# Handing the row maxima of an attention softmax to the padded q by transfers of one element per partition

## The chip, the cores and the metric

The kernel runs on one core of a Trainium2 chip. A core has five engines that each work through their own queue of instructions: PE (the matrix unit; its weight loads are listed apart as PEld), DVE (vector), ACT (activations and copies), POOL and SP, which here only issues transfers. Sixteen DMA engines move the data. The engines meet at semaphores. The metric is the device time of one execution in microseconds; lower is better.

## The reference

The input x has 8 sequences of 1024 tokens with 256 features. Two blocks follow each other, each with a layer norm before and after and a residual around it:

```python
x = x + layernorm(attention(layernorm(x), Wq, Wk, Wv, Wo))
x = x + layernorm(experts(layernorm(x), router, gate_up, down, biases))
```

The attention has 16 heads of 16 features, is causal and scales the scores by 1/4:

```python
score = where(causal, q @ k.T / 4, -inf)      # per sequence and head, 1024 x 1024
attn  = softmax(score, axis=-1)
out   = attn @ v
```

The second block sends each token to the best 2 of 8 experts (512 inner features). It is not touched by the change.

## The kernel before, in words

**Two stages.** The attention stage runs to about 1340 us, the expert stage after it. The change lies wholly in the first.

**Turns.** A turn u is one sequence b and one group g of four heads: 8 x 4 = 32 turns, `b, g = divmod(u, NG)`. The four heads lie on the partitions in bands of 32 rows: `qP` (the padded q) and `kP` hold in each band 16 rows of features and, in row 16 (`hh * HS + DH`), one row more. In `kP` that row is 1. In `qP` it is first 0 and later minus the maximum of each query's scores, so that the same matmul that makes the scores also subtracts the maximum. There are three such pairs of buffers, taken in turn (`u % NU`).

**Two passes over the scores.** The softmax needs each query's maximum before the exponentials. The first pass (`maxima_tiles`, matmul at line 831, tile `sa`) makes the scores with the queries on the partitions, 128 queries a block, eight blocks a turn, and reduces them to maxima on DVE (lines 841 to 866, 885) in the tile `mx`. The second pass (`values_tiles`, line 926, tile `sb`) makes them again with the keys on the partitions, now with the maximum in row 16; ACT takes the exponential (line 938, `pT`), POOL masks the diagonal blocks, PE multiplies by the values (line 967, `av`).

**Steps.** Each pass has nine steps k (`STEPS`, lines 773 to 784), and the loop at line 1309 runs the first pass of turn u and the second pass of turn u - 1 side by side, step by step, in two halves (a pair of heads each). Queries come in two chunks c of 512 (four blocks each). All first-pass scores of chunk 0 are done with step 2. Of chunk 1, blocks 4 to 6 are done with step 7 and block 7 with step 8, the last. The second pass of the next turn reads chunk 0's row at its step 0 and chunk 1's row in the second part of its step 2.

**From maxima to rows.** Between lies `rows(c)` (line 794): DVE takes the last maximum over three partial ones and negates it (line 797, `nm`, 128 queries x 4 heads x 4 blocks), PE transposes that into 16 partitions of 128 (line 800, `nmps`), ACT copies it to SBUF (line 802, `nmT`), and four transfers on SP's queue (line 804) put four rows of 128 for each head into row 16 of that head's band.

**Who orders the work.** In this stage the order on PE, DVE, ACT and SP is the order in which the program emits it. The matmuls of the steps stand fixed; everything else is a job that yields pieces with a cost per engine, and `pump` (line 1250) emits a piece after each half step if its engines have credit. `rows` is an urgent job, begun by `counted_off` (line 870) when the last step of its chunk is done; whatever is not yet emitted when the second pass needs it is forced out at lines 1312 to 1314. `after=1` holds a piece back for one half step more.

**SP's queue.** SP works strictly in order: a transfer that waits holds all behind it. Besides the rows it issues `spread` (lines 754 to 766: two transfers of zeros into the rows 16 of a band and eight that spread q and k into a pair of buffers, for the next turn), the outputs of `normalize` into `aT` (line 1007, four for each turn and chunk), the loads of x, the stores of the first block's result (line 1049), and in the last turn four early loads for the expert stage (`load_early`, line 1280). A transfer also waits until the eighth before it has landed, since eight semaphores go round. `finish` multiplies `aT` by the output weights (line 1028, `yps`).

## Time and profile before

| | us |
|---|---|
| median of 13 runs | 2152.26 (2148.81 to 2157.28) |
| the profiled execution | 2153.21 |
| its span | 2151.5 |
| PE busy | 2069.8 (96%) |
| DVE busy | 1668.1 (78%) |
| ACT busy | 1070.2 (50%) |
| POOL busy | 1051.3 (49%) |
| transposes of the maxima (line 800) | 64 at 0.277 |
| copies of them (line 802) | 64 at 0.249 |
| issues of row transfers on SP (line 804) | 256 at 0.578 |

The profile is of one execution. A group's line names the source line, engine, operation, the tiles written and read, the count and the durations in ns. A line of the time line gives the start, the duration in us, the instruction, how many were merged, and in brackets how long its engine sat idle before it and what ended that. On SP the duration is that of the issue alone; the data move after it.

### The profile page before, as it was taken

What the parts mean: (1) busy time and instruction counts of PE and PEld (TensorE: products, weight loads), DVE (VectorE), ACT (ScalarE), POOL (GpSimd) and SP (SyncE); (2) the same over time, 40 slices, a digit from 0 to 9 for tenths busy, and PEclk for the clock granted to TensorE, in tenths of its full rate; (3) what the DMA queues carried; (4) which work ended last, traced back from release to release, by engine and by line L of the source; (5) the groups of instructions that cost most, each with busy time, mean ns of one, the idle gap of its engine ahead of it and who ended that gap; (6) DMA issues with size and microseconds to landing.
All of it is one profiled execution on the core that took longest, in us unless ns stands there. A gap on an engine that the chain in (4) does not pass through costs nothing.

```text
span 2151.5 us, 44512 instructions
## 1 busy us (share of the span) xinstructions
PE 2069.8 (96%) x16269; PEld 1272.5 (59%) x16269; DVE 1668.1 (78%) x3834; ACT 1070.2 (50%) x2132; POOL 1051.3 (49%) x1216
## 2 busy tenths in 40 slices
PE   7999999999999999999999999899999999999995
PEld 4344444444444444445444444688888888888884
DVE  4676887878786888798787798378778888877776
ACT  3566665666666666666666666333122323232222
POOL 3321563474274365556455355455544445444443
PEclk9999999999999999999999999999999999999998
DMA  4102102112111121211211111656876877777774
GB/s 129 19 9 49 27 29 69 40 35 50 37 48 43 40 58 40 58 46 39 57 39 46 29 54 44 209 179 223 265 248 232 280 273 257 256 243 247 268 278 147
DMA packets 147095, 254.85 MB, mean 118 GB/s; under 512 B 21504, under 2 KB 106008, under 8 KB 144952
## 3 DMA queue, kind: packets, MB, share of 16 engines
q1 hardware_dynamic: 133128, 217.01, 32.9%
q0 software_dynamic: 12528, 34.36, 4.3%
q8 instruction: 130, 2.13, 0.4%
q14 instruction: 93, 0.76, 0.1%
q10 hardware_dynamic: 1216, 0.58, 0.1%
HBM read 171.13 MB, written 55.63 MB: 105 GB/s over the span
## 4 chain that ended last, share of the span: by engine, by line
PE 76%; DVE 13%; POOL 5%; issue 2%; DMA 2%; ACT 2%; SPq 0%; ACTq 0%; DVEq 0%; POOLq 0%
PE sa L831 20%; PE gu L1458 14%; PE av L967 12%; PE dn L1498 8%; PE sb L926 7%; PE yps L1028 3%; PE pjk L738 3%; PE pjq L738 3%; PE vps L724 3%; DVE acc L1573 1%; POOL ytd L1511 1%; DVE act L1479 1%; DVE gate L1467 1%; DVE up L1471 1%; PE xtps L1436 1%
## 5 line engine op out<-in xcount | busy, mean ns | idle before, releaser
L938 ACT ACTIVATE pT<-sb 128x512 f32<-128x512 f32 x1134 | 616.4, 595 | 363.8 <-PE sb L926 347.4
L926 PE MATMUL sb<-qP,kP 32*128 32x512 f32 (+3 forms) x3072 | 710.5, 522 | 3.3 <-DMA qP<-nmT 3.0
L831 PE MATMUL sa<-kP,qP 32*128 32x512 f32 (+3 forms) x3072 | 651.6, 523 | 9.5 <-DVE mx L841 3.8
L1458 PE MATMUL gu<-xsT,wg 128*128 128x256 f32 (+1 forms) x2208 | 487.7, 374 | 6.0 <-DMA wg<-_L_ffn_gate_up_proj_dram 4.1
L1458 PEld LDWEIGHTS gu<-xsT,wg 128*128 128x128 f32 x2208 | 410.1, 191 | 60.6 <-issue 4.8
L947 POOL TENSOR_SCALAR_AFFINE_SELECT pT<-pT 128x512 f32<-128x512 f32 x256 | 161.0, 644 | 500.7 <-ACT pT L938 475.5
L847 DVE TENSOR_REDUCE mx<-sa 128x2 f32<-128x1024 f32 x256 | 311.5, 1219 | 98.6 <-PE sb L926 93.1
L1469 ACT ACTIVATE sig<-gate 128x256 f32<-128x256 f32 (+1 forms) x276 | 112.8, 409 | 533.1 <-DVE gate L1467 528.5
L831 PEld LDWEIGHTS sa<-kP,qP 32*128 32x128 f32 x3072 | 226.8, 184 | 209.5 <-issue 88.8
L967 PE MATMUL av<-pT,vpad 128*32 128x256 f32 (+1 forms) x5120 | 347.8, 367 | 1.1 <-DVE avs L978 0.9
L1474 POOL TENSOR_TENSOR sig<-sig,gate 128x256 f32<-128x256 f32 (+1 forms) x276 | 198.1, 721 | 258.1 <-ACT sig L1469 256.1
L926 PEld LDWEIGHTS sb<-qP,kP 32*128 32x128 f32 x3072 | 299.9, 184 | 39.8 <-ACT pT L938 10.8
L967 PEld LDWEIGHTS av<-pT,vpad 128*32 128x32 f32 x5120 | 115.8, 109 | 290.9 <-issue 220.9
L1498 PE MATMUL dn<-wd,act 128*128 128x256 f32 x1064 | 258.9, 382 | 17.7 <-DVE act L1479 17.1
L1498 PEld LDWEIGHTS dn<-wd,act 128*128 128x128 f32 x1064 | 194.4, 190 | 51.0 <-DVE act L1479 29.1
L1467 DVE TENSOR_SCALAR gate<-gu,bs 128x256 f32<-128x256 f32 (+1 forms) x276 | 129.0, 468 | 121.4 <-PE gu L1458 95.6
L841 DVE CUSTOM_DVE_ANT_0 sa<-sa,cmask 128x512 f32<-128x512 f32 x256 | 178.2, 698 | 53.9 <-PE sb L926 35.5
L1511 POOL DMA_INDIRECT ytd<-ys,places x133 | 133.8, 1006 | 126.1 <-DVE ys L1506 94.0
L1191 POOL DMA_INDIRECT xsd<-xn,slots x128 | 128.1, 1001 | 48.3 <-issue 30.4
L1479 DVE SCALAR_TENSOR_TENSOR act<-up,sig 128x256 f32<-128x256 f32 (+1 forms) x276 | 125.7, 455 | 25.1 <-POOL sig L1474 25.1
L885 DVE TENSOR_REDUCE mx<-edge 128x8 f32<-128x1024 f32 x96 | 116.0, 1208 | 20.5 <-POOL edge L880 20.3
L866 ACT COPY edge<-sa 128x512 f32<-128x512 f32 x192 | 113.1, 589 | 34.1 <-DVE mx L862 20.0
(244 smaller groups left out, 2327.0 us busy)
## 6 DMA issues: line engine op xcount, KB each, us to landing
wg<-_L_ffn_gate_up_proj_dram SPq DMA_DIRECT2D x69, 1024.0 KB
wd<-in_L_ffn_down_proj_dram SPq DMA_DIRECT2D x69, 512.0 KB
xs<-xsd SPq DMA_DIRECT2D x60, 258.0 KB
yy<-ytd SPq DMA_DIRECT2D x15, 1024.0 KB
bs<-biasd SPq DMA_DIRECT2D x69, 132.0 KB
x<-in_L_attn_x_dram SPq DMA_DIRECT2D x16, 512.0 KB
aT<-avn SPq DMA_DIRECT2D x256, 32.0 KB
x1d<-y SPq DMA_DIRECT2D x16, 512.0 KB
```

The lines of the kernel that those rows point to most:

```text
L831: nc.tensor.matmul(ps[:, hh, ds(at, w)], lhsT=qP[r, ts(i, P)], rhs=kP[r, ds(c * QC, w)], start=True, stop=True,)
L841: nc.vector.tensor_tensor_reduce(out=ps[:, hh, :], in0=ps[:, hh, :], in1=cmask, scale=1.0, scalar=NEG, op0=ALU.add, op1=ALU.max, accum_out ...
L847: nc.vector.tensor_reduce(mx[:, heads, i, 2:3], ps, AX.X, ALU.max)
L926: nc.tensor.matmul(banks[hh][:, ds(at, QC - off)], lhsT=kP[r, ts(j, P)], rhs=qP[r, ds(c * QC + off, QC - off)], start=True, stop=True,)
L938: nc.scalar.activation(pT[:, 2 * pair + hh, :], banks[hh], AF.Exp)
L947: in_order(nc.gpsimd.affine_select(out=d, in_=d, compare_op=ALU.is_ge, fill=0.0, base=0, pattern=[[0, HG], [1, P]], channel_multiplier=-1,))
L967: nc.tensor.matmul(av[ds(hh * HS, HS), ds(off + a - at, z - a)], lhsT=vp[:, j, ds((g * HG + hh) * VS, HS)], rhs=pT[:, hh, a:z],  start=c n ...
L1458: nc.tensor.matmul(ps[:, half, :w], lhsT=wg[:, kt, ds(half * FF + f * P, P)], rhs=xT[:, kt, :], start=(kt == 0), stop=(kt == KT - 1),)
L1467: nc.vector.tensor_scalar(gt, ps[:, 0, :w], bs[:, f : f + 1], LIMIT, ALU.add, ALU.min)
L1474: in_order(nc.gpsimd.tensor_tensor(sg, sg, gt, ALU.mult))
L1498: nc.tensor.matmul(pss[n][:, 0, :], lhsT=act[:, f, ts(n, P)], rhs=wd[:, f, :], start=(f == 0), stop=(f == FT - 1),)
L1511: put = nc.gpsimd.indirect_dma_start(out=yt_dram[:, :], out_offset=bass.IndirectOffsetOnAxis(ap=places[:, i, n : n + 1], axis=0), in_=y[:, ...
```

## The change

`rows` now works on three groups in place of two chunks: chunk 0, blocks 4 to 6 of chunk 1, and block 7. It no longer transposes. After the reduction (`nm`, 128 queries on 128 partitions) each block of each head leaves by a transfer of its own that takes one 4-byte element from each of 128 partitions and puts them side by side into row 16: 16 transfers for chunk 0, 12 and 4 for chunk 1. The transpose, its PSUM tile, the copy and the tile `nmT` are gone, and so is the half step for which the second piece was held back. The first of chunk 1's groups is begun after step 7, the other after step 8. `rows_of` holds a list of jobs for each chunk.

```diff
--- before.py
+++ after.py
@@ -791,27 +791,32 @@
             mx = mxs[u % 2]
             edges = {}
 
-            def rows(c):
+            def rows(group):
+                c, blocks = GROUPS[group]
                 yield piece(dve=0.2)
-                nm = ap2.tile([P, HG, n], F32, tag="nm", name=f"nm_{u}_{c}")
-                nc.vector.tensor_reduce(nm, mx[:, :, ts(c, n), :], AX.X, ALU.max, negate=True)
-                yield piece(pe=0.15, act=0.3, after=1 if u else 4)
-                ps = ps_b.tile([HG * n, P], F32, tag="b", name=f"nmps_{u}_{c}")
-                nc.tensor.transpose(ps, nm.rearrange("p h i -> p (h i)"), ident)
-                nmT = ap2.tile([HG * n, P], F32, tag="nmT", name=f"nmT_{u}_{c}")
-                nc.scalar.copy(nmT, ps)
-                for hh in range(HG):
-                    nc.sync.dma_start(
-                        out=qP[hh * HS + DH : hh * HS + DH + 1, ts(c, QC)].rearrange(
-                            "o (i q) -> o i q", q=P
-                        ),
-                        in_=nmT[ts(hh, n), :],
-                    )
-
-            left = [
-                sum(c in {i // n for i, _, _ in tiles} for _, tiles, _ in STEPS)
-                for c in range(NC)
-            ]
+                m = len(blocks)
+                nm = ap2.tile([P, HG, m], F32, tag=f"nm{m}", name=f"nm_{u}_{group}")
+                nc.vector.tensor_reduce(
+                    nm, mx[:, :, ds(c * n + blocks[0], m), :], AX.X, ALU.max, negate=True
+                )
+                yield piece()
+                for i in range(m):
+                    for hh in range(HG):
+                        r = hh * HS + DH
+                        nc.sync.dma_start(
+                            out=qP[r : r + 1, ds(c * QC + (blocks[0] + i) * P, P)],
+                            in_=nm[:, hh, i : i + 1],
+                        )
+
+            GROUPS = [(0, range(n)), (NC - 1, range(n - 1)), (NC - 1, range(n - 1, n))]
+
+            def groups_of(k):
+                return {
+                    g for g, (c, blocks) in enumerate(GROUPS)
+                    if any(i // n == c and i % n in blocks for i, _, _ in STEPS[k][1])
+                }
+
+            left = [sum(g in groups_of(k) for k in range(K)) for g in range(len(GROUPS))]
 
             def of_two(k):
 
@@ -868,10 +873,12 @@
                 return scores, reduce
 
             def counted_off(k):
-                for c in {i // n for i, _, _ in STEPS[k][1]}:
-                    left[c] -= 1
-                    if not left[c]:
-                        rows_of[u, c] = start(urgent, rows(c))
+                for g in sorted(groups_of(k)):
+                    left[g] -= 1
+                    if not left[g]:
+                        rows_of.setdefault((u, GROUPS[g][0]), []).append(
+                            start(urgent, rows(g))
+                        )
 
             def masked_edges(k):
 
@@ -1310,8 +1317,9 @@
                     if second:
 
                         for c in {t[0] for t in STEPS[k][2]}:
-                            while not rows_of[u - 1, c].done:
-                                emit(urgent, rows_of[u - 1, c])
+                            for job in rows_of[u - 1, c]:
+                                while not job.done:
+                                    emit(urgent, job)
                     if u == B * NG - 1 and not early and NT - LATE in known:
                         load_early()
                     if first and g == 0 and b + 1 < B and k == 5:
```

## The prediction

> **What bounds the kernel now.** I read the page first (busy shares, groups, DMA issues), then the table by stretch, then the instructions of the tiles nm, nmps and nmT, the chain, and last the time line around one handing-over of maxima.

> ```profile
> span 2151.5 us, 44512 instructions
> PE 2069.8 (96%) x16269; PEld 1272.5 (59%) x16269; DVE 1668.1 (78%) x3834; ACT 1070.2 (50%) x2132; POOL 1051.3 (49%) x1216
> ...
> PE 76%; DVE 13%; POOL 5%; issue 2%; DMA 2%; ACT 2%; SPq 0%; ACTq 0%; DVEq 0%; POOLq 0%
> ```
> ```profile
> 400.00:700.00 300.00, 295.24 (x2857) 140.13 (x2852) 240.28 (x497) 191.31 (x369) 163.98 (x179) 1.00 0.18 44
> 700.00:1000.00 300.00, 297.24 (x2850) 140.68 (x2848) 248.83 (x551) 189.00 (x367) 166.31 (x180) 1.00 0.19 47
> ```
> The columns are stretch, length, then PE, PEld, DVE, ACT, POOL busy, granted clock, DMA share, GB/s. In the attention stage (to about 1340 us, 32 turns of about 41 us) PE is busy for 98 to 99%, at full clock. Time taken from PE is time taken from the stage; time added to anything else costs only where it makes PE wait. The expert stage after it is not touched.

> What the change removes, and what the removed transfers cost:
> ```profile
> L797 DVE TENSOR_REDUCE nm<-mx x64: 158/200/204, 41.0 to 1331.7; 128x16 f32<-128x48 f32 x64
> L800 PE MATMUL nmps<-ident,nm x64: 269/277/278, 45.3 to 1332.5; 128*16 128x128 f32 x64
> L802 ACT COPY nmT<-nmps x64: 236/249/255, 45.6 to 1333.2; 16x128 f32<-16x128 f32 x64
> L804 SPq DMA_DIRECT2D qP<-nmT x256: 572/578/722, 45.9 to 1335.6; - x128
> ```
> Other transfers to compare the new ones with (min/median/max ns that SP is held for one issue): three from SBUF to SBUF, one from SBUF to DRAM in 1024 pieces of 32 bytes, one of 128 rows from DRAM:
> ```profile
> L759 SPq DMA_DIRECT2D qP<-zeros x58: 565/600/649, 88.5 to 1255.1; - x58
> L762 SPq DMA_DIRECT2D qP<-unq x132: 526/583/1668, 17.8 to 1257.7; - x132
> L1007 SPq DMA_DIRECT2D aT<-avn x256: 507/582/2742, 85.9 to 1373.5; - x128
> L693 SPq DMA_DIRECT2D biasd<-bias x1: 527/527/527, 37.0 to 37.0; - x1
> L1419 SPq DMA_DIRECT2D bs<-biasd x69: 332/346/1832, 1358.9 to 2110.4; - x69
> ```
> One handing-over, turn 6, from three answers of the time line (DVE, SP, weight loads):
> ```profile
> 294.69 1.23 DVE L847 TENSOR_REDUCE mx<-sa 128x2 f32<-128x1024 f32 x1 [0.68 <-PE sb L926]
> ...
> 298.43 1.23 DVE L847 TENSOR_REDUCE mx<-sa 128x2 f32<-128x1024 f32 x1 [0.44 <-PE sb L926]
> 299.69 0.20 DVE L797 TENSOR_REDUCE nm<-mx 128x16 f32<-128x48 f32 x1
> ```
> ```profile
> 302.14 2.66 SPq L804 DMA_DIRECT2D qP<-nmT  x4
> ```
> ```profile
> 309.29 0.19 PEld L926 LDWEIGHTS sb<-qP,kP 32*128 32x128 f32 x2
> ```
> The seventh block's maxima (step 7) end at 295.92, the eighth's at 299.66; the rows are issued from 302.14 to 304.80 and first read at 309.29, 13.4 us after the end of step 7. Read the same way, the first read comes 10.9 to 14.7 us after step 7 in turns 1 to 30 (six of them within 10.9 to 11.1). Only in turns 0 and 31 do the weight loads wait long for the rows; the last wait shows how late a row lands, 1.08 us after the last issue ended at 1336.17:

> ```profile
> 69.07 0.49 PEld L926 LDWEIGHTS sb<-qP,kP 32*128 32x128 f32 x2 [3.38 <-DMA qP<-nmT]
> ...
> 1337.25 0.29 PEld L926 LDWEIGHTS sb<-qP,kP 32*128 32x128 f32 x2 [0.37 <-DMA qP<-nmT]
> ```

> **The change part by part.**

> *PE, off.* 64 transposes. 64 x 0.277 = 17.7 us is the upper end. In the chain from 296 to 345 us line 800 holds 1.3% of 49 us, 0.64 us for three transposes: 0.21 us each, as their start overlaps the matmul before. 64 x 0.21 = 13.4 us is the lower end while PE stays the bound. I take 14.

> *ACT, off.* 64 copies, 15.9 us. ACT is busy for 63 to 64% of this stage, and its copy lay beside PE's work: 0. Should PE's queue ever wait for ACT there, it is a gain of under 1 us.

> *DVE, on.* Three reductions in place of two a turn. By 0.20 us for 48 elements and 0.158 at the least, the two smaller ones take 0.15 to 0.19 each: +0.15 us a turn, 4.8 us busy. DVE holds 13% of the chain: +0.6 us; ends 0 and 4.8.

> *SP, on.* 256 issues become 1024: 16 for chunk 0, then 12 and 4 for chunk 1. By the four SBUF-to-SBUF rows an issue holds SP for 0.578 to 0.600 us; the bounds are 0.346 (128 rows from DRAM) and 0.722 (the worst of line 804). I take 0.59, since the new ones are SBUF to SBUF too. SP then issues some 204 transfers in four turns, 120 of 166 us: it is no bound as a whole, but the bursts matter.

> *Chunk 1 (the tight one).* The instruction order of the new program puts group 1's reduction right behind the last one of step 7, and both groups ahead of the next spread of q and k, behind which the old rows stood. Group 1 can be issued 0.6 us after step 7 (a 0.2 us reduction and hand-overs). Twelve issues end at 0.6 + 12 x 0.59 = 7.7 us; group 2's maxima are ready at 3.7 to 5.1, so its four follow at once and end at 10.0. With 1.08 us to land, the rows are there 11.1 us after step 7: on time in every turn, by 3.6 us at most and by nothing in the six tight ones (a head read 0.2 us later needs the last issue; that makes up for the 0.2 us that PE comes earlier). The lateness against the read, summed over turns 1 to 30 (0.6 + 16 issues + 1.08, less the read): nothing at 0.58 us an issue, 1 at 0.60, 9 at 0.65, 21 at 0.70, 34 at 0.75, 97 at 0.90. I take +1. The turns that end a batch start group 1 behind the spread of ten transfers; for turn 11 (chunk 0 from 486.1: 16 + 4 + 10 issues end at 504.3) the rows land at 514.8, the read is at 515.7.

> *Waits that go.* PE and its loads now wait 8.8 us, eight times, for the rows, 4.1 of it (3.38 and 0.72) in turn 0, whose rows stood behind a spread. There step 7 ends at 55.4, so the new rows land at 66.5 in place of 69.07: -2.6 us. I take -3, ends 0 and -8.8.

> *Turn 31.* Here the new order puts the four early loads of the expert stage between groups 1 and 2; they took 3.76 us of SP before. Rows then land at about 1328.0 + 7.1 + 3.8 + 2.4 + 1.08 = 1342.4 instead of 1337.25: +5 us, ends 0 and +10.

> *Behind chunk 0.* Its 16 issues are queued ahead of aT's four. In turn 4 they end at 197.3 + 9.6 = 206.9 instead of 202.1, so aT is out at 209.3; its projection starts at 211.7, 1.3 us after the landing. The other fifteen projections have 3.2 to 17 us. Cost 0; from 0.7 us an issue on it is no longer nothing. The spread that follows has half a turn and more: 0.

> *Landing.* The one thing the trace has no row for is 128 pieces of 4 bytes that go into one partition. L693's 1024 pieces of 32 bytes started within 0.73 us, so 128 need about 0.1 us; its packets took 7.8 ns each. If instead all 128 went in one after the other, it would be 1.0 us: landing 1.0 later, some 11 us of waits at 0.59. I take 0, ends 0 and +11.

> [...]

> Sum: -14 + 0.6 + 1 - 3 + 5 = -10.4. The profiled execution took 2153.2 us (span 2151.5), 0.9 above the median of 2152.3. 2153.2 - 10.4 = 2142.8; against the median 2141.9. I say 2142.

> **The rivals.**

> *Cheap issues.* An issue takes the 0.346 us of L1419. Then no row is ever late: -17.7 - 8.8 + 0.6 = 2127. For it: equally 128 pieces. Against: every SBUF-to-SBUF row is at 0.58.

> *Hidden.* PE's free slots fill with other waits, because DVE (80 to 83% busy) sets the pace of those steps: 2152. For it: DVE's 13% of the chain. Against: PE's 98 to 99%.

> *Slow landing.* One partition takes the pieces singly, or landing grows by 1.6 us: 19 us of waits, 2142 + 19 = 2161.

> *SP late (the slower side).* The issue of an element-wise transfer is dearer than of any row here. It decides at about 0.65 us: there waits cancel the gain. At 0.75 it is 2142 + 33 = 2175, at 0.90 2238, and by 0.82 (50 issues in 41 us) SP is the bound of the stage. For it: the chunk-1 margin is 0 in six turns. Against: L693, at 0.527 for 1024 pieces.

> **How the numbers follow.** Forecast 0.45 (its own range 2134 to 2149), cheap issues 0.15, hidden 0.10, slow landing 0.10, SP late 0.20, half of it above 2185. The range 2126 to 2185 leaves out that half and a twentieth below. This kernel's measurement can tell about 0.2% (4.3 us) from no change. Faster: 0.42 + 0.15 = 0.57; same: 0.03 + 0.08 = 0.11; slower the rest, 0.32.

> **What would show it.** Right: PE has 64 matmuls fewer, its busy share of the stage stays at 98%, SP's new issues are at 0.55 to 0.62 us, and sb's waits for qP stay under 10 us in all. Wrong: SP's element-wise issues over 0.65 us, waits of PE on qP from nm in most turns, waits of yps for aT, or a landing over 2 us after the issue's end.

## The result, and the profile after

The changed kernel takes 2201.24 us (median; 2198.5 to 2206.4), the kernel before beside it 2151.08 us. The ratio is 1.0234, with a 95% interval of 1.0222 to 1.0245: slower, by 2.3%. The prediction was 2142 us with a range to 2185; sign and range are both missed. The profiled execution's span grew from 2151.5 to 2201.5 us, so the +50.0 us can be followed in the trace.

The page of the kernel after: span, busy time of each engine, and the shares of the chain that ended last.

```profile
span 2201.5 us, 45760 instructions
PE 2082.1 (95%) x16205; PEld 1277.6 (58%) x16205; DVE 1670.2 (76%) x3866; ACT 1063.7 (48%) x2068; POOL 1053.9 (48%) x1216
...
PE 68%; DVE 15%; POOL 7%; issue 3%; DMA 3%; SPq 2%; ACT 1%; ACTq 0%; DVEq 0%; POOLq 0%
```

PE ran 64 matmuls fewer, as it should, and was nevertheless busy for 12 us more. In the chain, DMA and SP's queue have gone from 2% to 5%. The two stretches that the prediction showed, and then two short ones (length, then busy time of PE, PEld, DVE, ACT, POOL, granted clock, DMA share, GB/s):

```profile
400.00:700.00 300.00, 291.56 (x2762) 137.92 (x2754) 237.42 (x509) 184.72 (x344) 162.90 (x177) 0.98 0.23 42
700.00:1000.00 300.00, 292.52 (x2815) 137.46 (x2818) 239.91 (x528) 186.82 (x350) 149.43 (x165) 0.99 0.23 43
```
```profile
211.00:217.00 6.00, 4.95 (x34) 2.62 (x34) 0.92 (x1) 1.46 (x3) 0.00 (x0) 0.72 0.01 3
1360.00:1375.00 15.00, 7.06 (x82) 3.31 (x73) 2.28 (x6) 5.51 (x9) 5.51 (x7) 0.79 0.35 81
```

PE is idle for 8 us in 300 instead of 3 to 5, and the clock column, 1.00 in both stretches before, has dropped: a busy PE now is sometimes a PE at half clock. The short stretches show it: from 211 us the clock is 0.72, just after a wait for aT; from 1360 us it is 0.79, around the wait of turn 31. PE's time line there shows the wait and what half clock costs: 16 matmuls of one kind (av) take 1.07 us ahead of it and 1.94 us behind it.

```profile
1361.72 1.07 PE L974 MATMUL av<-pT,vpad 128*32 128x256 f32 x16
...
1371.37 1.82 PE L933 MATMUL sb<-qP,kP 32*128 32x256 f32 x8 [7.94 <-DMA qP<-nm]
1373.12 1.94 PE L974 MATMUL av<-pT,vpad 128*32 128x256 f32 x16
```

The waits of PE in the kernel after (in total, how often, the longest) show for what:

```profile
PE sb L933 <- DMA qP<-nm: 19.9, 17, 7.9
...
PE yps L1035 <- DMA aT<-avn: 7.8, 5, 2.6
PE sa L836 <- DVE mx L846: 7.5, 11, 1.8
PE segps L363 <- DVE new L354: 6.0, 1, 6.0
...
PE sa L836 <- DMA kP<-unk: 3.2, 2, 1.7
```

For rows (sb) PE waited 3 us before, for aT (yps) not at all. Why they are late is on SP. First the group of row transfers and the reductions (min/median/max ns), then SP's time line around turn 7:

```profile
L806 SPq DMA_DIRECT2D qP<-nm x1024: 468/552/1824, 42.6 to 1369.9; - x171
L799 DVE TENSOR_REDUCE nm<-mx x96: 158/166/198, 41.4 to 1359.2; 128x16 f32<-128x48 f32 x32, 128x12 f32<-128x36 f32 x32, 128x4 f32<-128x12 f32 x32
```
```profile
300.81 10.42 SPq L806 DMA_DIRECT2D qP<-nm  x16
316.06 3.43 SPq L1014 DMA_DIRECT2D aT<-avn  x4
324.50 10.96 SPq L806 DMA_DIRECT2D qP<-nm  x16
335.56 2.46 SPq L1014 DMA_DIRECT2D aT<-avn  x4
```

An issue is recorded with 0.552 us, less than the old rows' 0.578. But sixteen of them take 10.4 to 11.0 us: from start to start it is 0.643 us in the median over the whole trace, 0.68 in the mean. That difference is at the core of the late rows.

I split each stage of the trace into PE's idle time, half of the time in which PE was busy at half clock (an estimate: what such a stretch costs if work takes twice as long in it; the 16 matmuls above took 1.94 us for 1.07), and the rest, which I call work:

| us | length | PE idle | half clock | work |
|---|---|---|---|---|
| attention before | 1329.0 | 22.1 | 4.1 | 1302.8 |
| attention after | 1366.5 | 53.3 | 22.0 | 1291.2 |
| experts before | 766.0 | 25.1 | 4.3 | 736.6 |
| experts after | 778.3 | 32.4 | 8.2 | 737.7 |

So a gain near the predicted one is there, 11.6 us of work; waits took 31.2 and half clock 17.9 in the attention stage, and 12.3 more went in the expert stage, whose code is the same. The work is what is left over, and it holds more than the transposes: in e6 below, which leaves out the same 64, it fell by 25 us. How much of the 11.6 us is theirs is not shown.

### The profile page after: what moved, and what is told of

It is laid out like the page before. It is cut to its first block, busy times and chain, and to the rows that moved or that the text cites. A ratio compares the mean times of both kernels' runs of the same rounds, so it can differ in the third digit from the quotient of the medians.

```text
span 2201.5 us, 45760 instructions
## 1 busy us (share of the span) xinstructions
PE 2082.1 (95%) x16205; PEld 1277.6 (58%) x16205; DVE 1670.2 (76%) x3866; ACT 1063.7 (48%) x2068; POOL 1053.9 (48%) x1216
## 4 chain that ended last, share of the span: by engine, by line
PE 68%; DVE 15%; POOL 7%; issue 3%; DMA 3%; SPq 2%; ACT 1%; ACTq 0%; DVEq 0%; POOLq 0%
PE sa L836 17%; PE gu L1466 14%; PE av L974 10%; PE dn L1506 7%; PE sb L933 6%; PE pjq L738 3%; PE yps L1035 3%; PE pjk L738 2%; DVE mx L852 2%; PE vps L724 2%; DVE acc L1581 1%; POOL pT L954 1%; POOL xsd L1198 1%; POOL ytd L1519 1%; DVE act L1487 1%
## 5 line engine op out<-in xcount | busy, mean ns | idle before, releaser
L933 PE MATMUL sb<-qP,kP 32*128 32x512 f32 (+3 forms) x3072 | 717.3, 529 | 20.3 <-DMA qP<-nm 19.9
L836 PE MATMUL sa<-kP,qP 32*128 32x512 f32 (+3 forms) x3072 | 658.8, 528 | 19.0 <-DVE mx L846 7.5
L933 PEld LDWEIGHTS sb<-qP,kP 32*128 32x128 f32 x3072 | 303.2, 187 | 56.0 <-DMA qP<-nm 17.9
L1479 DVE TENSOR_SCALAR up<-gu,bs 128x256 f32<-128x256 f32 (+1 forms) x276 | 128.3, 465 | 0.0
```

Source lines behind the costliest of these rows:

```text
L836: nc.tensor.matmul(ps[:, hh, ds(at, w)], lhsT=qP[r, ts(i, P)], rhs=kP[r, ds(c * QC, w)], start=True, stop=True,)
L933: nc.tensor.matmul(banks[hh][:, ds(at, QC - off)], lhsT=kP[r, ts(j, P)], rhs=qP[r, ds(c * QC + off, QC - off)], start=True, stop=True,)
```

## The experiments

Theory: SP issues one of the new transfers each 0.643 us; bursts of twelve and sixteen make what stands behind them late (rows, aT, the spread), and waits of PE bring stretches at half clock. Rivals: the 4-byte pieces are slow themselves; the number of transfers is too large; one place (turn 31) does it all.

**e3: sixteen transfers without 4-byte pieces.** The kernel before with each row of 512 bytes sent by itself.

```diff
-for hh in range(HG):
-    nc.sync.dma_start(out=qP[...ts(c, QC)]..., in_=nmT[ts(hh, n), :])
+for i in range(n):
+    for hh in range(HG):
+        nc.sync.dma_start(out=qP[r : r + 1, ds(c * QC + i * P, P)],
+                          in_=nmT[hh * n + i : hh * n + i + 1, :])
```

> The kernel before, with its transposes and copies, but each row of 512 bytes leaves by a transfer of its own: 16 issues a chunk in place of 4, no 4-byte pieces. Theory (SP's bursts come late: 16 issues take 10.2 us and more, and the rows, aT and the spread behind them miss their readers): at least as slow as the changed kernel, 2200 to 2225 us, since the rows also start some 2 us later behind the transpose; PE idle in the attention stage 50 us or more (22 before), and more stretches of half clock. Rival (the 4-byte pieces into one partition are what is slow): nothing changes, 2150 us within 6.

Measured: 2472.41 us, ratio 1.1486 (1.1449 to 1.1523), start to start 0.632 us. The mean granted clock is 0.928. From the waits of this run:

```profile
PE sb L926 <- DMA qP<-nmT: 193.0, 33, 10.4
```

Far worse than expected, since all sixteen of chunk 1 stand behind step 8 and behind the spread. It has no 4-byte piece in it: lateness comes of the number of issues in a row. And it prices a wait: PE's idle time in the stage grew by 196.4 us over the kernel before, the loss to half clock by 113.2 us, 0.58 us on top of each us waited; the changed kernel has 0.57 (17.9 on 31.2). In e4, e5 and e6, with 11 to 15 us of added waits, it is 0.8, 0.4 and 0.2.

**e4 and e5: one chunk each in the old way** (one transpose, one copy, four transfers). In e4 it is chunk 0; in e5 it is chunk 1, as one group.

```diff
 def rows(group):
     c, blocks = GROUPS[group]
+    if c == 0:      # e5: c == 1
+        ...         # reduction, transpose, copy and four transfers as before
+        return
```

> The changed kernel with chunk 0's rows by transpose, copy and four transfers as before; chunk 1 leaves by 12 and 4 element-wise transfers. Theory (bursts): nothing stands long ahead of aT and the spread any more, so the projection's waits for aT (7.8 us) go and the waits of sa for the spread too; what stays is chunk 1's lateness, 5 to 12 us, with half the gain on PE (6 us): 2150 to 2172 us. Rival (4-byte pieces): half the pieces, half the loss, 2170 to 2182.

> The changed kernel with chunk 1's rows by transpose, copy and four transfers in one group, behind the spread as before; chunk 0 leaves by 16 element-wise transfers. Theory (bursts): the projection still waits for aT (5 to 10 us), the spread at the end of a batch is late for sa, rows of chunk 1 behind that spread too; half the gain on PE: 2160 to 2185 us. Rival (only chunk 1's rows matter, as the prediction had it): 2145 us, the gain alone.

Measured: e4 2180.36 us, 1.0138 (1.0105 to 1.0171); e5 2152.75 us, 1.0002 (0.9989 to 1.0015). Their waits, e4's first:

```profile
PE sb L951 <- DMA qP<-nm: 13.3, 11, 3.3
...
PE yps L1053 <- DMA aT<-avn: 2.1, 2, 1.8
```
```profile
PE yps L1053 <- DMA aT<-avn: 5.3, 4, 2.4
PE sb L951 <- DMA qP<-nmT: 3.3, 2, 3.0
```

In e4, with chunk 1's bursts alone, the rows are late and aT nearly on time; in e5, with chunk 0's burst alone, aT is late and the rows are as before (3.3 us). Chunk 1 is the dearer one; e5 as a whole ends where the kernel before does. The times fit the theory less well than the waits: e4 lies in the range of its rival (half the pieces, half the loss) and e5 7 us under the range of the theory. What decides against the pieces is e6.

**e6: the same 1024 transfers in eight groups of one block.**

```diff
-GROUPS = [(0, range(n)), (NC - 1, range(n - 1)), (NC - 1, range(n - 1, n))]
+GROUPS = [(i // n, range(i % n, i % n + 1)) for i in range(NB)]
```

> The changed kernel with eight groups in place of three: each block of 128 queries leaves by its own reduction and four element-wise transfers as soon as its step is done. The same 1024 transfers and pieces, no burst over 4 to 8; five more small reductions a turn on DVE. Theory (bursts): rows, aT and spread are on time again, the sum is the gain on PE of 12 us less 4 for DVE: 2140 to 2160 us. Rival (number of transfers or of pieces as such): 2195 us or more.

Measured: 2149.35 us, 0.999 (0.9975 to 1.0006). No wait of sb for rows, none of yps for aT. SP's time line of e6 at the same place as above:

```profile
301.39 2.41 SPq L806 DMA_DIRECT2D qP<-nm  x4
307.97 2.46 SPq L1014 DMA_DIRECT2D aT<-avn  x4
310.54 8.24 SPq L806 DMA_DIRECT2D qP<-nm  x12
318.87 2.46 SPq L1014 DMA_DIRECT2D aT<-avn  x4
322.94 6.32 SPq L806 DMA_DIRECT2D qP<-nm  x8
```

Same count, same pieces, 52 us less than the changed kernel: neither the 4-byte pieces nor the total of issues is the cause. It does not win clearly. PE now waits 26.4 us at sa (9.5 before), 17.6 of it for DVE, which has 256 small reductions of 0.159 us; that these make it wait was not tried by itself.

All runs that follow were made where the kernel before took 2202 to 2207 us, so only their ratios and their traces among each other are compared. To see what is different there, and what the change costs there:

**e11, e16 and e15: the changed kernel, the kernel before and e6, each unchanged.**

> The changed kernel itself, unchanged, beside the runs that follow, because the kernel before took 2207 us where e7 to e10 ran and 2152 us elsewhere. If the loss is in the order of the work on SP, the ratio is again near 1.023 and the waits of sb for rows near 20 us. Rival: it depends on the chip, and the ratio is the 1.015 that e7 and e9 showed, or less.

> The kernel before, unchanged, for a profile beside the others of this call: its waits for rows and its half-clock windows. Where it takes 2207 us, 55 us more than elsewhere: if that is PE waiting at places that have nothing to do with the rows (half clock with them), the waits of sb for rows are as in the first profile, 3 us, and the comparison within one call stands. Rival: the rows themselves land later on that chip: 10 us or more of waits for rows in this kernel too.

> The run block by block (ratio 0.999) once more, beside the changed kernel on one chip: the same transfers in eight groups. If bursts are the cause on any chip, the ratio stays at 0.996 to 1.003 while that of the changed kernel is 1.015 to 1.025. Rival: it was the chip, and both move together.

Measured: e11 2238.52 us, 1.0144 (1.0119 to 1.017); e16 0.9999 (0.9987 to 1.0011); e15 2212.62 us, 1.003 (1.0016 to 1.0044). Waits for rows in e16, then in e11:

```profile
PE sb L926 <- DMA qP<-nmT: 3.3, 3, 3.0
```
```profile
PE sb L933 <- DMA qP<-nm: 15.1, 10, 8.3
...
PE yps L1035 <- DMA aT<-avn: 6.0, 5, 3.0
```

The rows are as punctual in e16 as in the first profile. Its attention stage is 46.5 us longer all the same: 12.3 more PE idle, at places where the trace shows no cause, 20.2 more half clock, 14.0 more of the rest. What stalls PE there stays open. The change's own waits are nearly those of the first profile (31.0 us more idle in e11 than in e16, 31.2 there). Its cost is 31 us here against 50; that half clock grows by 11.5 us and not by 17.9 is one part of this, the rest is open. e15 is again faster than e11, but by 1.1% and not by 2.4%; it has again no wait for rows or aT, and three waits of 6.5 us at sb, whose cause its trace does not show, are new in it.

**e7: turn 31's early loads behind the last rows.**

```diff
-if u == B * NG - 1 and not early and NT - LATE in known:
-    load_early()
```

> The changed kernel with one thing moved: in turn 31 the four early loads are issued behind the last four row transfers and no longer between them and the twelve. If the wait of 7.94 us at 1363.4 us is set by what stands on SP ahead of the last four, these start at 1363.7 instead of 1367.95 us: the wait falls by about 4.2 us, and the 3.4 us of half clock behind it may go with it (1.7 us): about 2195 us. Rival: the loads, now 2.5 us later, hold up the first expert tile by as much, or the wait is one for the twelve: 2199 to 2201 us.

Measured: ratio 1.0145 (1.0121 to 1.0169), that of e11: the time did not tell. The wait did. SP's time line of the changed kernel in turn 31, then that of e7:

```profile
1355.84 7.85 SPq L806 DMA_DIRECT2D qP<-nm  x12
1364.78 3.06 SPq L1287 DMA_DIRECT2D early<-xsd  x4
1367.95 2.45 SPq L806 DMA_DIRECT2D qP<-nm  x4
```
```profile
1389.25 10.43 SPq L806 DMA_DIRECT2D qP<-nm  x16
1400.76 3.78 SPq L1287 DMA_DIRECT2D early<-xsd  x4
```

The wait there is 2.49 us in e7 and 8.35 in e11: 5.9 us of it were the loads. No gain in time came of it: PE's idle time at sb is 30.4 us in e7 and 31.2 in e11, since other waits of e7 are longer (3.3 us near 606 us and 4.1 near 787 us, 1.7 and 2.1 in e11), put down to ACT or to nothing that the trace shows.

**e9: the second tile table out of its lump.** In the changed kernel the list of leftover work is later, and the rest of it, the second tile table, is emitted in one piece when the expert tiles have got to the fourteenth. PE waits 6.0 us at segps and 3.1 at tabps for it, and a stretch at half clock follows at 1583.7 us.

```diff
-pump(1.2, 1.4, 1.0, 0.7)
+pump(1.5, 1.7, 1.2, 0.9)
```

> The changed kernel, attention as it is; only the shares by which the list of leftover work is mixed into the first expert tiles are larger (1.5, 1.7, 1.2, 0.9 for 1.2, 1.4, 1.0, 0.7), so that the second tile table is made among the expert tiles and not in one lump at tile 14. If the experts' stage got 12.3 us longer because the table's 9.1 us of PE waits (6.0 at segps, 3.1 at tabps) and the half clock behind them came in that lump, the stage goes from 778.3 back to 766 to 770 us and the time to 2189 to 2193 us. Rival: the stage is longer for another reason, by the clock alone or by late loads: 776 us or more, 2199 us or more.

Measured: 1.0153 (1.0138 to 1.0169). The expert stage takes 774.5 us; it takes 776.4, 776.1 and 779.6 in e7, e10 and e11, which have the lump. Waits in e9:

```profile
PE cps L1157 <- DVE chosen L1153: 5.4, 3, 3.4
PE tabps L417 <- DVE two L414: 3.8, 1, 3.8
...
PE segps L363 <- DVE new L354: 0.2, 1, 0.2
```

The wait at segps went, others came; 2 to 5 us of the 12.3 are explained, far from the 8 to 12 that were expected. Over all kernels tried, the expert stage took 761 to 780 us with the same code (but for e9). What it inherits from the attention stage's order I have not settled.

**e10: chunk 0's sixteen in four portions**, two half steps apart; chunk 1 as in the changed kernel.

```diff
 for i in range(m):
+    if i and not c:
+        yield piece(after=2)
     for hh in range(HG):
```

> The changed kernel with chunk 0's sixteen transfers in four portions of four, two slots apart; chunk 1's twelve and four as they are, the work on PE, ACT and DVE the same. If the burst of sixteen behind chunk 0 is what held up aT, the spread and x1d on SP, the waits at yps go from 7.8 us to under 1, those at sa from 19.0 to about 12, and half-clock windows go with them: 2178 to 2186 us. Rival: all of the loss is that of chunk 1's rows (sb 20.3 us and the half clock behind these waits): 2197 to 2201 us.

Measured: 1.0099 (1.008 to 1.0117), 0.0045 under e11.

```profile
PE sb L935 <- DMA qP<-nm: 18.0, 13, 8.1
...
PE yps L1037 <- DMA aT<-avn: 1.8, 1, 1.8
```

aT's waits nearly went, the rows' stayed. Of the 18.0 us, 3.2 are for chunk 0's own rows, which the portions now bring too late; in the changed kernel these never made PE wait. The gain, about 10 us, is half of what was expected.

**e8, e18, e12 (with its repeat e17) and e13: chunk 1 by blocks, chunk 0 in three ways.** e18 regroups chunk 1 of the changed kernel into four groups of one block; e8 does that and takes e10's portions for chunk 0; e12 does it with chunk 0 in the old way (that is, e4 with chunk 1 by blocks); e13 is e12 with chunk 1 in groups of two, one and one.

```diff
-GROUPS = [(0, range(n)), (NC - 1, range(n - 1)), (NC - 1, range(n - 1, n))]
+GROUPS = [(0, range(n))] + [(NC - 1, range(i, i + 1)) for i in range(n)]
 # e13:   [(0, range(n))] + [(NC - 1, r) for r in (range(2), range(2, 3), range(3, 4))]
```

> The changed kernel with chunk 0's sixteen transfers in four portions of four, two slots apart, from one reduction, and chunk 1's in four groups of one block, each with its own reduction behind the step that completes the block: 160 small reductions on DVE instead of 96 (after) or 256 (block by block). If late rows and bursts are all that the change cost, there are no waits of sb for rows and none of yps for aT, as in the run block by block (2149.4 us). If in addition the 26.4 us in which PE waited at sa in that run came of DVE's 256 reductions of 0.159 us, 96 fewer are 15.3 us less on DVE and about a third of that comes off: 2142 to 2146 us. Rival: the waits at sa are those for the large reductions and for the slots, whatever the small ones do: 2149 us. A burst that matters even in portions would give over 2155 us.

> The changed kernel with only chunk 1 regrouped, four groups of one block; chunk 0's burst of sixteen stays. It differs from e12 in chunk 0 alone (16 transfers of 4-byte pieces for a transpose, a copy and 4 transfers). If chunk 0's burst costs what e4 and e10 suggest (aT, spread and x1d held up on SP), it is 0.005 to 0.02 above e12, below the changed kernel by the waits of sb for rows: 1.000 to 1.010. Rival: chunk 0's burst costs nothing, and the ratio is at or under that of e12.

> The run with chunk 0 in the old way (e4_chunk0_old, 2180.4 us, ratio 1.0138) with one thing changed: chunk 1's sixteen transfers leave in four groups of one block, each behind its step, and not as twelve and four. Same transposes (32), same transfers. If the two bursts of chunk 1 are the whole loss of that run, the 13.6 us of waits of sb for rows and the half clock behind them go: 32 transposes fewer than before are worth 32 x 0.22 = 7 us, 96 reductions more on DVE of 0.159 us are 15.3 us on an engine that PE waits for now and then; a ratio of 0.996 to 1.002. Rival: 4-byte pieces in chunk 1 cost something in every grouping: over 1.008.

> e12 once more: ratio 0.9896 where before took 2207 us. If the gain is that of the PE work and the missing waits, 0.990 to 0.998 on any chip; where before takes 2152 us, 2131 to 2148 us. Rival: the 0.9896 was mostly that before suffers more from the chip: 0.998 to 1.002 where before takes 2152 us.

> As e12, with chunk 1 in three groups, of two blocks, one and one: 32 reductions fewer on DVE, eight transfers behind step 6 (8 x 0.643 = 5.1 us of SP, a step is 4.6 us) and four behind each of the last two. The last four land as in e12 if SP is free by step 8, which it is by this sum. Then 0.995 to 1.001, at or under e12. Rival: eight in a row already hold up the spread and the last four: over 1.004.

| | chunk 0 | chunk 1 | ratio (95%) | PE's waits for transfers in the stage |
|---|---|---|---|---|
| e8 | 4 portions | 4, 4, 4, 4 | 1.027 (1.0243 to 1.0297) | kP 15.3 us, rows of chunk 0 12.7 |
| e18 | 16 | 4, 4, 4, 4 | 1.0075 (1.0055 to 1.0094) | kP 25.7 us, aT 2.6 |
| e13 | old | 8, 4, 4 | 1.0107 (1.009 to 1.0123) | kP 14.3 us, rows 0.3 |
| e12 | old | 4, 4, 4, 4 | 0.9896 (0.9879 to 0.9913) | none |
| e17 | old | 4, 4, 4, 4 | 0.9896 (0.9878 to 0.9914) | none |

Regrouping chunk 1 took its rows off the path, and in e18, e8 and e13 something else on SP came late: the spread, kP and qP of the next turn. (e13 also waits once for aT, 11.0 us, in the expert stage.) In e18 SP's time line and PE's at the same place:

```profile
340.65 5.03 SPq L806 DMA_DIRECT2D qP<-nm  x8
345.74 1.32 SPq L759 DMA_DIRECT2D qP<-zeros  x2
347.16 2.46 SPq L762 DMA_DIRECT2D qP<-unq  x4
349.73 2.43 SPq L762 DMA_DIRECT2D kP<-unk  x4
```
```profile
352.16 1.71 PE L836 MATMUL sa<-kP,qP 32*128 32x512 f32 x2 [6.07 <-DMA kP<-unk]
```

Eight row transfers, 5.0 us, stand ahead of the ten of the spread, and PE waits 6.07 us for kP, the last four of these. e8 and e13 have the same new wait; of both I had expected a ratio of 1.001 or less, having counted only whether the rows of chunk 1 land in time. In e12 SP has twelve transfers a turn less to issue than in e18, and PE waits for none of them. The number alone does not decide it: e6 and e15 issue as many as e18 and wait 3.3 and 0.2 us for kP; what differs is how the program's order mixes rows and spread. e12 is a version that beats both kernels, 1.0% under the kernel before there, and again in e17. Where the kernel before takes 2152 us it was not run; how much of its lead is the other's half clock there (24.3 us in e16, 15.6 in e12, 6.1 in e17) is open.

**Half clock and waits.** Over the seventeen traces, from 80 to 1330 us, I counted PE's idle stretches and the half-clock windows that begin within 5.5 us of a stretch's start:

| idle stretch, us | count | followed by a window |
|---|---|---|
| 0.4 to 0.8 | 185 | 19 (10%) |
| 0.8 to 1.2 | 118 | 17 (14%) |
| 1.2 to 1.8 | 73 | 31 (42%) |
| 1.8 and more | 96 | 80 (83%) |

Of all 141 windows 126 have an idle stretch of 0.8 us or more ahead of them. The windows last 3.4, 6.8, 10.2 or (three of them) 13.7 us, one to four times 3.41. It is a count over traces and not an experiment with the wait alone; but e3, where only transfers were split, took the count of windows in this stretch from none to 27.

The edges of the windows lie on one grid of 3.413 us in each trace, and by the cells of this grid the count is sharper. Of the cells at full clock with 2.0 us or more of PE idle in them, all 53 were followed by half clock; with 1.2 to 2.0 us it was 49 of 94, with 0.4 to 1.2 us 32 of 351, and with less 2 of 5417.

What the clock follows beyond PE's idle time, and why the edges keep to such a grid, no run shows.

## Why the prediction was wrong, step by step

- **SP, on** (failed; the mechanism was named, the size was wrong). The prediction took 0.59 us an issue, the time for which the record holds SP. What counts is from start to start: 0.643 in the median, 0.68 in the mean. Its own lines showed this: four rows of before in 2.66 us are 0.665 each, not 0.578. The sixteen of chunk 1 took 10.2 to 11.7 us in turns 1 to 30, where 9.4 were forecast. With 0.65 its own table gives 9 us of row waits, with 0.70 it gives 21. Measured: 19.9 in all, 12.0 without the 7.9 of turn 31. The table was right and was entered at the wrong place. Of the 12.0, 3.7 fell in the seven turns that end a batch, where the twelve started 2 to 6 us late behind the spread; the prediction had gone through turn 11 alone, at no cost (measured 0.1). What fills the 0.09 us between the 0.552 recorded and the 0.643 from start to start, no run shows. SP's strict order and its eight semaphores show in the kernel before: at the row transfers SP stood 369.2 us in all for nmT, in 45 waits of up to 14.1 us, with nothing issued meanwhile, and at 1375.9 us it stood 2.3 us until the eighth transfer before, a load of wg issued at 1366.17, had landed.
- **Turn 31** (right mechanism, undersized). Predicted +5 us, measured 7.9; by e7 against e11, 5.9 of such a wait are the four early loads and 2.5 the rows themselves.
- **Waits that go** (right). The wait of turn 0 fell from 2.98 us of PE to 0.15; predicted -3.
- **Behind chunk 0** (failed). "Cost 0" became 7.8 us at yps, and the spread that "has half a turn and more" was late too (3.2 us at sa for kP; 25.7 in e18). In turn 4, which the prediction worked out, SP was not later than it said:

```profile
194.70 10.48 SPq L806 DMA_DIRECT2D qP<-nm  x16
205.23 1.14 SPq L230 DMA_DIRECT2D x<-in_L_attn_x_dram  x2
206.47 2.47 SPq L1014 DMA_DIRECT2D aT<-avn  x4
```

The last issue for aT ended at 208.94, forecast 209.3. Two other terms were wrong. PE stood waiting from 209.44 and not from 211.7, as its projection came 3.0 us earlier than in the kernel before; the prediction had kept the old time of the read. And aT was taken to land like a row, 1.1 us after its last issue; PE went on at 212.06, 3.1 us after it. The two loads of x just ahead of aT, 512 KB each, kept the DMA engines at work from 206.5 to 210.4, and aT's packets ran from 209.4 to 211.0. In four of the five waits for aT two loads of x stand there.

- **Left out altogether.** The sum priced a wait at its own length. Many waits of over a microsecond brought half clock as well (over all traces 31 of 73 idle stretches of 1.2 to 1.8 us and 80 of 96 longer ones were followed by it): +17.9 us in the attention stage. And the expert stage, "not touched", became 12.3 us longer, partly because the change of jobs also moved the leftover work there.
- **PE, off** (right as far as it can be told). 11.6 us of work gone, predicted 14; see above for what that work holds. **ACT, off**: predicted 0, and nothing in the runs speaks against it. **DVE, on** (undersized or not, open): predicted +0.6 us with an end at 4.8; PE's waits at sa for DVE grew from 6.1 to 13.9 us, and no run shows how much of this is the third reduction. **Landing** (right): in turn 31 the last issue ends at 1370.40 and PE goes on at 1371.37, 0.97 us later, against 1.08 for the old rows. The 4-byte pieces, for which the prediction held up to 11 us open, cost nothing that e6 or e12 could show (no wait for rows in either, ratios 0.999 and 0.9896).

The sum, then: against the predicted -10.4 the span moved by +50.0. Of the 60.4 between them, 28.2 are PE's waits in the attention stage (31.2, against the +3 of the three waiting terms), 17.9 its half clock, 12.3 the expert stage, 1.8 the smaller gain of work; 0.2 lie at the two ends of the span. By place, PE's idle time grew by 17.0 us at sb, 9.5 at sa and 7.8 at yps and fell by 3 elsewhere.

The rival that came nearest is "SP late". Its condition, waits that cancel the gain from 0.65 us on, was met by the spacing and not by the recorded duration. Its reason was not: an element-wise issue is no dearer than others (0.643 us, 0.626 for those of unq, 0.68 for the old rows). And its price was too low as well: by the prediction's table 0.68 us an issue makes about 2157 us, as it counts the waits for rows alone. "Slow landing" and "cheap issues" are out; against "hidden" speak the 11.6 us.

## What to carry to other kernels

Price an issuing queue by the time from one issue to the next in a burst, not by the recorded duration of one (here 0.643 us, not 0.552), and ask of every burst what stands behind it: here rows, aT, spread and early loads all came late in turn, and moving one wait uncovered the next. The small transfers were cheap where each group left as soon as its part was ready and the queue had room (no wait for rows in e6 and e12, but 25.7 us for kP in e18); the best version split only the chunk that was tight. Where PE is the bound, count waits at their length and, as an estimate from these runs, about half more for the half clock that follows (17.9 on 31.2 us of added waits in the changed kernel, 113.2 on 196.4 in e3; 0.2 to 0.8 us on each in e4 to e6).
